# Attention and non-local layer: key differences renewed by a transfer or from the keys, a denser prologue, and a ScalarE copy of layer 1's denominators

## The chip, the cores and the metric

The program runs on one core of a Trainium2 chip. The metric is the device time of one execution in microseconds (us), as a median over runs. The engines are called as in the profile: PE (TensorE, matmuls), DVE (VectorE), ACT (ScalarE), POOL (GpSimd), SP (SyncE, which here only issues transfers). POOL and ACT issue transfers too.

## The reference

Two layers follow each other, all in float32, on x of 2 x 256 x 64 x 64 (two batches, 256 channels, 4096 positions).

```python
# layer 0: attention over 8 heads of 32 channels
qkv = jnp.einsum('oc,bchw->bohw', w_qkv, x)
q, k, v = map(reshape, jnp.split(qkv, 3, axis=1))        # b, 8, 32, 4096
scores = jnp.einsum('bhdi,bhdj->bhij', q, k) / sqrt(32)
out = jnp.einsum('bhij,bhdj->bhdi', softmax(scores), v)
x = jnp.einsum('oc,bchw->bohw', w_proj, out) + x
# layer 1: non-local block
g_x = maxpool2(conv1x1(x, g_w, g_b))                      # 256 channels, 1024 positions
theta_x = conv1x1(x[:, :64], theta_w, theta_b)            # 64 channels, 4096 positions
phi_x = maxpool2(conv1x1(x[:, 64:], phi_w, phi_b))        # 64 channels, 1024 positions
y = softmax(theta_x^T phi_x) applied to g_x
x = batchnorm(conv1x1(y, W_w, W_b)) + x
```

## The kernel before

**Tiling.** The eight heads of a batch are two quads of four heads (32 channels each, so a quad fills 128 partitions). `QUAD` counts them n = 0 to 3 over both batches: n = 0, 1 are batch 0, n = 2, 3 batch 1. A quad's 4096 queries are eight blocks of 512 (i = 0 to 7), and within a block a loop runs over 32 chunks of 128 keys (j = 0 to 31). For each block and j: `score` (line 452) makes the scores of the chunk in PSUM, ACT takes the exp (line 598) in two pairs of heads, `weigh` (line 476) multiplies the weights with v, and `add` sums the weights for the denominators: pair 0 by POOL (line 509, line 518 for the last chunk), pair 1 two chunks at a time by a transfer of 1 MB that adds in memory, issued by POOL (line 515). A block's two transferred sums are folded into one by another such transfer (line 524) and an addition (line 528), early in the next block. The weights stand in two rotating sets of buffers: `single` (six, for pair 0) and `double` (five, each two chunks of pair 1, or a running sum).

**Differences of keys.** The scores stay in PSUM from chunk to chunk: the matmul of chunk j adds q times the difference between chunk j's keys and those of the chunk before. In `keys` order the chunks walk over the eight stretches of 512 keys, so the differences needed are those between neighbouring stretches c = j % 8: odd c in `kd` (1, 3) and `last_kd` (5, 7), even c in `mid_kd` (2, 4, 6), and c = 0 in `turn_kd`. `kd` has two buffers; the other three have one and are renewed for the next quad when the last block of the quad before has read them for the last time. `between` makes one of mid_kd's three parts (128x512) on POOL, `rounds` makes turn_kd on POOL, `differences` makes one part of kd, first_kd or last_kd on POOL. `before_all` makes last_kd's content for the next quad early, in a tile `first_kd`, because the maxima (below) need it while the old last_kd is still read. `renew` does the renewals: mid_kd in the last block at j = 26, 28 and 30, turn_kd in the first block at j = 2, and two ACT copies first_kd to last_kd in the first block at j = 0 and 2.

first_kd has the tag "x" of a pool with one buffer, which the loads of x for q, k and v (x_q, x_k) and, at a batch's end, the weights of the projection and of two convolutions (`late_weights`, lines 103 to 107) also use.

**Maxima.** `maxima` finds the row maxima of the scores for a block ahead of its attention: about 4 chunks more than a block ahead. `plain` makes a product (line 293) that DVE reduces (line 305). `pair` uses differences: ACT takes a Relu of q times the difference (line 313), and DVE adds it to a product and reduces (line 320), which covers two stretches. The very first block's maxima are made by `first_block` in 33 slots, in the prologue, each with four products, two Relus (line 358) and two of DVE's joint reductions. `make_rows` turns finished maxima into rows by transposes on PE (line 150), which are subtracted in PSUM at j = 0 of a block (line 464).

**Prologue.** Ahead of the attention the program makes k, v and q of quad 0 from x (`make`, lines 185 and 197); these are the dense items, 14 of them after the first k, k, q. Four slots of the maxima follow each of k 2 to 7, v 0 and v 1; then come q(0,1) and v 2 to 7, with one step of the next block's maxima each.

**Batch end and layer 1.** `project` multiplies by w_proj (line 639), DVE adds x (line 646, from loads x_res, line 88, in `single` buffers); halfway it makes the last block's denominators (`den`, line 536). `non_local` makes theta, phi and g (lines 676 to 710) and then, per block of 512 positions i and for t = 0 to 3: scores (line 805), exp (line 820), the accumulation into two PSUM tiles (y, line 771) and sums on POOL (lines 763, 767), with maxima of later blocks (products line 739, reductions line 746) between. `result` then makes the denominators in a PSUM tile `den` (line 783), the reciprocal on DVE (line 785), and the output (lines 787, 790). The PSUM tiles y, y, den and pt (transposes) rotate over four buffers, and the program's waits follow the order in which they are given back.

**What sets the order.** The text of the loops gives the order; a scheduling layer orders each engine's instructions by priority, so that an instruction can stand earlier than in the text, and sets semaphores. `tc.issue_after` keeps an instruction behind another in that order.

Of the kernel before, what the change touches and what calls it, by code (L numbers as in the profile page):

```python
# [19 lines left out]
QUADS = HEADS // QH  # L20
# [5 lines left out]
NI = N // NB  # L26
NJ = N // P
# [8 lines left out]
def conv_attention(  # L36
# [13 lines left out]
    nc = tc.nc  # L50
# [116 lines left out]
    QUAD = [(b, qd) for b in range(B) for qd in range(QUADS)]  # L167
    q, k, v, kd = {}, {}, {}, {}
    held = {}

    def make(what, n, i):
        b, qd = QUAD[n]
        if (b, i) not in held:
            name = f"x_{what}_{n}_{i}"
            held.clear()
            held[b, i] = load_x(b, i, xs.tile([P, NC, NB], F32, tag="x", name=name))
        xc = held[b, i]
        name = f"{what}_{b}_{qd}_{i}"
        pq = scratch(name)
        if what == "v":  # L180
            if i == 0:
                v[n] = qkv.tile([P, NJ, QH, D], F32, tag="v", name=f"v_{n}")
            for j in range(NB // P):
                for c in range(NC):
                    nc.tensor.matmul(  # L185
                        pq[:, bass.ts(j, P)],
                        xc[:, c, bass.ts(j, P)],
                        wv_sb[:, c, bass.ts(qd, P)],
                        start=(c == 0),
                        stop=(c == NC - 1),  # L190
                    )
                if j % 2 == 1:
                    yield
            nc.scalar.copy(v[n][:, bass.ts(i, NB // P)].rearrange("p j h d -> p (j h d)"), pq)
            return
        for c in range(NC):
            nc.tensor.matmul(  # L197
                pq,
                wqk_sb[:, c, qd, 0 if what == "q" else 1, :],
                xc[:, c, :],  # L200
                start=(c == 0),
                stop=(c == NC - 1),
            )
            yield
        if what == "q":
            to = q[n, i] = qkv.tile([P, NB], F32, tag="q", name=f"q_{n}_{i}", bufs=3)
        else:
            if i == 0:
                k[n] = qkv.tile([P, N], F32, tag="k", name=f"k_{n}")
            to = k[n][:, bass.ts(i, NB)]  # L210
        nc.scalar.copy(to, pq)
        if what == "k" and i % 2 == 0 and i > 0 and n == 0:
            between(n, i // 2 - 1)
        if what == "k" and i == NI - 1 and n == 0:
            rounds(n)
        if what == "k" and i % 2 == 1 and n == 0:
            if i == 1:
                kd[n] = qkv.tile([P, NI // 4, NB], F32, tag="kd", name=f"kd_{n}")
            differences(n, i // 2, (kd[n] if i < NI // 2 else last_kd)[:, i // 2 % (NI // 4), :])
# [5 lines left out]
    def differences(n, c, to):  # L225
        two = k[n][:, bass.ts(c, 2 * NB)]
        nc.gpsimd.tensor_sub(to, two[:, NB:], two[:, :NB])
# [6 lines left out]
    def between(n, c):  # L234
        two = k[n][:, NB * (2 * c + 1) : NB * (2 * c + 3)]
        nc.gpsimd.tensor_sub(mid_kd[:, c, :], two[:, NB:], two[:, :NB])

    def rounds(n):
        nc.gpsimd.tensor_sub(
            turn_kd,  # L240
            k[n][:, P:NB].rearrange("p (a n) -> p a n", n=P),
            k[n][:, N - NB : N - P].rearrange("p (a n) -> p a n", n=P),
        )

    def renew(i, j, n):


        if (i, j) == (NI - 1, NJ - 6):
            between(n + 1, 0)
        elif (i, j) == (NI - 1, NJ - 4):  # L250
            between(n + 1, 1)
        elif (i, j) == (NI - 1, NJ - 2):
            between(n + 1, 2)
        elif (i, j) == (0, 2):
            rounds(n)
        if i == 0 and j in (0, 2):
            nc.scalar.copy(last_kd[:, j // 2, :], first_kd[n][:, j // 2, :])

# [146 lines left out]
    def advance(steps, n=1):  # L407
        for _ in range(n):
            next(steps, None)
# [3 lines left out]
    def make_rows():  # L413

        for i, r in enumerate(rows):
            if callable(r):
                if i in seen:
                    rows[i] = r()
                seen.add(i)


    def attend(b, y):
# [153 lines left out]
        for qd in range(QUADS):  # L576
            for i in range(NI):
                blk = Block(qd, i)
                items = during(blk.n, i)
                both = [None, None]  # L580
                for j in range(NJ):
                    if j % 2 == 0:
                        two = double(f"p_{blk.name}_{j}_1")
                    p = [single(f"p_{blk.name}_{j}_0"), two[:, j % 2]]
                    for pair in (1, 0):
                        if j == 0:
                            s = both[pair] = scores(f"s_{blk.name}_{j}_{pair}")
                            subtract(s, pair, blk)
                            advance(maxes)
                            score(s, pair, blk, j)  # L590
                        else:
                            s = both[pair]
                            score(s, pair, blk, j)
                            advance(maxes)
                        with ExitStack() as order:
                            if cut is not None:
                                order.enter_context(tc.issue_after(cut.ins))
                            nc.scalar.activation(p[pair], s, AF.Exp, scale=scale)  # L598
                    if waiting is not None:
                        weigh(*waiting)  # L600
                        if j == 0:
                            normal = normalize(waiting[0])
                    add(blk, j, p, two)
                    waiting = blk, j, p
                    if j in (1, 5) or j >= AFTER:
                        advance(normal)
                    if j % 2 == 0:
                        make_rows()
                        if i > 0 and blk.n + 1 < len(QUAD) or i == 0 and blk.n > 0:
                            with tc.issue_after(added.ins) if added else ExitStack():  # L610
                                renew(i, j, blk.n)
                        if i == NI // 2 and j in (12, 14) and blk.n + 1 < len(QUAD):
                            if j == 12:
                                kd[blk.n + 1] = qkv.tile(
                                    [P, NI // 4, NB], F32, tag="kd", name=f"kd_{blk.n + 1}"
                                )
                            with tc.issue_after(added.ins):
                                differences(blk.n + 1, j // 2 - 6, kd[blk.n + 1][:, j // 2 - 6, :])
                        if (i, j) == (NI - 1, 8) and blk.n + 1 < len(QUAD):
                            with tc.issue_after(added.ins):  # L620
                                before_all(blk.n + 1)
                    for item in items.get(j, ()):
                        if item[1] < len(QUAD):
                            advance(make(*item), 9)
# [28 lines left out]
    def non_local(b, y, theta_w, phi_w):  # L653
# [125 lines left out]
        def result(i):  # L779
            cols = bass.ts(i, NB)  # L780
            z = single(f"z_{b}_{i}")
            den = scratch(f"den1_{b}_{i}")
            nc.tensor.matmul(den, ones, acc[i][NC], start=True, stop=True)
            r = work.tile([P, NB], F32, tag="r", name=f"r1_{b}_{i}", bufs=1)
            nc.vector.reciprocal(r, den)  # L785
            for o in range(NC):
                nc.vector.scalar_tensor_tensor(
                    z[:, o, :], acc[i][o], bn_scale[:, o : o + 1], r, ALU.mult, ALU.mult
                )
                nc.vector.scalar_tensor_tensor(  # L790
                    z[:, o, :], z[:, o, :], bn_shift[:, o : o + 1], y[:, o, cols], ALU.add, ALU.add
                )
            nc.sync.dma_start(out=dst[:, :, cols], in_=z)
# [46 lines left out]
        held[0, i] = load_x(0, i, x0[:, :, bass.ts(i, NB)])  # L840
    for what, i in (("k", 0), ("k", 1), ("q", 0)):
        advance(make(what, 0, i), 3)
    for what, i in [("k", i) for i in range(2, NI)] + [("v", 0), ("v", 1)]:
        advance(make(what, 0, i), 3)
        advance(maxes, G)
    advance(maxes)
    advance(make("q", 0, 1), 3)
    for i in range(2, NI):
        advance(maxes)
        advance(make("v", 0, i), 3)  # L850
        if i in (3, 5):
            make_rows()
    advance(maxes, 2 * LEAD - NI + 2)
    held.clear()
    for b in range(B):
        y = big.tile([P, NC, N], F32, tag="y", name=f"y{b}")
# [58 lines left out]
```

## Time and profile before

| | |
|---|---|
| median of 3 runs | 3904.28 us (3903.01 to 3907.87) |
| profiled execution, own time | 3908.37 us |
| its span | 3906.6 us, granted clock 0.997 |
| PE busy | 3864.0 us (99%) |
| POOL busy | 3091.5 us (79%) |
| DVE busy | 2900.7 us (74%) |
| ACT busy | 2697.5 us (69%) |

Stages of the span, by the first exp of a quad and the first or last matmul of a stage: prologue to 99.3; quad 0 to 912.4; quad 1 to 1729.0; projection to 1768.6; layer 1 of batch 0 to 2019.6; quad 2 to 2839.5; quad 3 to about 3611; projection and layer 1 of batch 1 to the end.

In the profile, "PEld" is PE's weight load, "SPq" or "POOLq" an issue by that queue. In a row of the timeline the first number is the start, the second the duration, and the bracket the idle time before with what ended it. In a row of the chain the two numbers are start and duration of a piece; a DMA piece is the time in which the chain waits for a transfer. In "who waited for it" the two numbers are us in total and times.

### The profile page before, as it was taken

To read this page: it belongs to the slowest core of one execution; us is meant where nothing else is said; L and a number is where in the kernel's file an instruction comes from. 1 tells how busy PE (TensorE), PEld (TensorE's weight loads), DVE (VectorE), ACT (ScalarE), POOL (GpSimd) and SP (SyncE) were. 2 spreads that over 40 slices of the span, in tenths; PEclk is the share of its full clock that TensorE was granted. 3 is DMA by queue.
4 is the path that set the end of the run, shared out by engine and by line. 5 is a ranking of instruction groups with operands and counts; after the bars stand their busy time and mean duration, and the time that the engine had idled before them with its cause. 6 is when DMAs were issued, how large, how long until landed. Compare 5 with 4: busy or idle time off the path is not lost.

```text
span 3906.6 us, 69965 instructions
## 1 busy us (share of the span) xinstructions
PE 3864.0 (99%) x27452; PEld 1366.8 (35%) x27452; DVE 2900.7 (74%) x5449; ACT 2697.5 (69%) x3378; POOL 3091.5 (79%) x1957
## 2 busy tenths in 40 slices
PE   9999999999999999999999999999999999999998
PEld 4333333333333333333333333333333333332333
DVE  5888888788888888764458888888888888884444
ACT  5787777777777777751137777777778888887111
POOL 1888899899989999871448899998999999997043
PEclk9999999999999999999999999999999999999999
DMA  1778878778878788780018888887788888889100
GB/s 57 145 167 169 172 166 170 168 162 172 168 167 169 166 168 169 167 188 6 22 34 169 168 175 168 173 171 164 163 176 171 170 170 170 168 168 188 53 17 27
DMA packets 112300, 566.26 MB, mean 145 GB/s; under 512 B 20200, under 2 KB 22504, under 8 KB 50784
## 3 DMA queue, kind: packets, MB, share of 16 engines
q0 software_dynamic: 68832, 501.25, 63.5%
q1 hardware_dynamic: 42448, 59.74, 4.5%
q8 instruction: 215, 3.52, 0.3%
q14 instruction: 117, 0.96, 0.1%
q10 hardware_dynamic: 688, 0.79, 0.1%
HBM read 51.63 MB, written 8.88 MB: 15 GB/s over the span
## 4 chain that ended last, share of the span: by engine, by line
PE 96%; DVE 2%; DMA 1%; POOL 1%; issue 0%; ACT 0%; DVEq 0%; POOLq 0%; ACTq 0%; SPq 0%
PE s L452 28%; PE w L476 26%; PE ps L293 23%; PE y L771 6%; PE q L197 2%; PE k L197 2%; PE v L185 2%; PE proj L639 1%; PE g L696 1%; DVE r L785 1%; PE f L739 1%; PE f L805 1%; PE den L536 1%; DMA p<-p 1%; PE tp L680 0%; PE tp L676 0%
## 5 line engine op out<-in xcount | busy, mean ns | idle before, releaser
L509 POOL TENSOR_TENSOR p<-p,p 128x1024 f32<-128x1024 f32 x945 | 2364.4, 2502 | 281.4 <-ACT p L598 262.7
L598 ACT ACTIVATE p<-s 128x1024 f32<-128x1024 f32 x2048 | 2087.6, 1023 | 560.5 <-PE ps L293 495.1
L293 PE MATMUL ps<-k,q 32*128 32x512 f32 x6142 | 2020.6, 626 | 2.5 <-DVE r L785 1.3
L305 DVE TENSOR_REDUCE part<-ps 128x1 f32<-128x512 f32 x2046 | 1315.7, 686 | 566.8 <-PE ps L293 563.1
L476 PE MATMUL w<-p,v 128*32 128x512 f32 x8192 | 1091.0, 605 | 1.1 <-ACT p L598 1.1
L452 PE MATMUL s<-q,mid_kd 32*128 32x512 f32 x3072 | 771.2, 615 | 0.0
L320 DVE CUSTOM_DVE_ANT_0 ps<-ps,over 128x512 f32<-128x512 f32 x1025 | 706.2, 691 | 24.9 <-PE ps L293 10.5
L491 DVE TENSOR_TENSOR y<-y,w 128x512 f32<-128x512 f32 x961 | 659.1, 686 | 51.9 <-PE w L476 49.3
L293 PEld LDWEIGHTS ps<-k,q 32*128 32x128 f32 x6142 | 625.1, 183 | 25.6 <-DVE part L320 10.4
L313 ACT ACTIVATE over<-ps 128x512 f32<-128x512 f32 x961 | 569.3, 592 | 10.7 <-PE ps L293 7.9
L293 PE MATMUL ps<-kd,q 32*128 32x512 f32 x1056 | 525.9, 593 | 0.0
L452 PE MATMUL s<-q,last_kd 32*128 32x512 f32 x2048 | 508.5, 615 | 4.5 <-ACT p L598 4.5
L452 PE MATMUL s<-q,kd 32*128 32x512 f32 x2048 | 510.5, 616 | 0.4 <-ACT p L598 0.3
L293 PE MATMUL ps<-last_kd,q 32*128 32x512 f32 x904 | 445.1, 590 | 0.0
L476 PEld LDWEIGHTS w<-p,v 128*32 128x32 f32 x8192 | 161.6, 108 | 805.3 <-DVE part L305 775.2
L452 PEld LDWEIGHTS s<-q,mid_kd 32*128 32x128 f32 x3072 | 270.4, 183 | 443.5 <-ACT over L313 253.9
L515 POOL DMA_DIRECT2D p<-p x448 | 395.3, 882 | 27.3 <-ACT p L598 27.1
L452 PEld LDWEIGHTS s<-q,kd 32*128 32x128 f32 x2048 | 174.0, 184 | 299.8 <-ACT over L313 182.7
L452 PEld LDWEIGHTS s<-q,last_kd 32*128 32x128 f32 x2048 | 172.8, 183 | 284.9 <-ACT over L313 178.5
L771 PE MATMUL y<-p,kv 128*128 128x512 f32 x512 | 240.1, 608 | 6.4 <-DVE r L785 6.4
L820 ACT ACTIVATE p<-f 128x1024 f32<-128x1024 f32 x64 | 65.5, 1023 | 248.5 <-PE f L805 219.2
L767 POOL TENSOR_TENSOR sums<-sums,p 128x512 f32<-128x512 f32 x96 | 121.3, 1264 | 113.7 <-ACT p L820 109.9
(120 smaller groups left out, 2806.3 us busy)
## 6 DMA issues: line engine op xcount, KB each, us to landing
p<-p POOLq DMA_DIRECT2D x478, 1024.0 KB, 7.6
x_q<-in_x_dram SPq DMA_DIRECT2D x30, 512.0 KB
x_k<-in_x_dram SPq DMA_DIRECT2D x24, 512.0 KB
x_res<-in_x_dram SPq DMA_DIRECT2D x16, 512.0 KB
out_dram<-z SPq DMA_DIRECT2D x16, 512.0 KB
r<-flat SPq DMA_DIRECT2D x120, 64.0 KB
x<-in_x_dram SPq DMA_DIRECT2D x8, 512.0 KB
wqk_sb<-in_wqk_dram ACTq DMA_DIRECT2D x1, 512.0 KB
```

Of the source, the lines that this page charges most:

```text
L197: nc.tensor.matmul(pq, wqk_sb[:, c, qd, 0 if what == "q" else 1, :], xc[:, c, :], start=(c == 0), stop=(c == NC - 1),)
L293: nc.tensor.matmul(ps, q[n, i][bass.ts(h, D), bass.ts(g, P)], keys[bass.ts(h, D), :], start=True, stop=True,)
L305: reduced = nc.vector.tensor_reduce(part[:, g, h, j : j + 1], ps, AX.X, ALU.max)
L313: cut = nc.scalar.activation(over, ps, AF.Relu)
L320: reduced = nc.vector.tensor_tensor_reduce(out=ps, in0=ps, in1=over, scale=1.0, scalar=LEAST, op0=ALU.add, op1=ALU.max, accum_out=part[:, ...
L452: nc.tensor.matmul(s[:, t, :], kj[bass.ts(h, D), :], q[blk.n, blk.i][bass.ts(h, D), :], start=False, stop=True, skip_group_check=j > 0,)
L476: nc.tensor.matmul(w[bass.ts(h, D), :], v[blk.n][:, keys(j), h, :], p[h // 2][:, h % 2, :], start=True, stop=True,)
L491: nc.vector.tensor_add(blk.num, blk.num, w)
L509: added = nc.gpsimd.tensor_add(blk.sums[0], blk.sums[0], p[0])
L515: sent = nc.gpsimd.dma_start(out=blk.sums[n], in_=two, accum_op=ALU.add)
L598: nc.scalar.activation(p[pair], s, AF.Exp, scale=scale)
L771: nc.tensor.matmul(acc[i][o], wg[:, 2 * t + j, bass.ts(o, P)], p[:, j, :], **edge)
```

## The change

`renew` is rewritten. When the next quad is of the same batch (n = 0 to 1 and 2 to 3), mid_kd's first two parts are made as before at j = 26 and 28 of the last block; at j = 30 SP issues a transfer of first_kd's first part to last_kd; at j = 0 of the next quad's first block SP issues the second part's transfer and POOL makes mid_kd's third part; turn_kd is made at j = 4. When the next quad begins a batch (n = 2), POOL makes all of them from k: mid_kd, turn_kd and both parts of last_kd, given in the text at j = 0 of the first block; in the program's order they stand on POOL in the last block of quad 1, each after the last reading of the part that it overwrites. The ACT copies are gone. In the prologue three slots go with each of eleven items (k 2 to 7, v 0 to 4), then q(0,1), three items with one step each (v 5 to 7), and five steps without an item. In `result`, ACT copies den to the SBUF tile r in blocks i = 0 to 6, and the reciprocal works in place on r.

```diff
@@ -245,16 +245,24 @@
     def renew(i, j, n):
-        if (i, j) == (NI - 1, NJ - 6):
-            between(n + 1, 0)
-        elif (i, j) == (NI - 1, NJ - 4):
-            between(n + 1, 1)
-        elif (i, j) == (NI - 1, NJ - 2):
-            between(n + 1, 2)
-        elif (i, j) == (0, 2):
+        b, qd = QUAD[n]
+        if i == NI - 1 and qd < QUADS - 1:
+            if j in (NJ - 6, NJ - 4):
+                between(n + 1, (j - NJ + 6) // 2)
+            elif j == NJ - 2:
+                nc.sync.dma_start(out=last_kd[:, 0, :], in_=first_kd[n + 1][:, 0, :])
+        elif i == 0 and j == 0 and n > 0:
+            if qd > 0:
+                nc.sync.dma_start(out=last_kd[:, 1, :], in_=first_kd[n][:, 1, :])
+                between(n, 2)
+            else:
+                for c in range(NI // 2 - 1):
+                    between(n, c)
+                rounds(n)
+                for c in range(2):
+                    differences(n, NI // 4 + c, last_kd[:, c, :])
+        elif (i, j) == (0, 4) and qd > 0:
             rounds(n)
-        if i == 0 and j in (0, 2):
-            nc.scalar.copy(last_kd[:, j // 2, :], first_kd[n][:, j // 2, :])
@@ -606,9 +614,8 @@
                         make_rows()
-                        if i > 0 and blk.n + 1 < len(QUAD) or i == 0 and blk.n > 0:
-                            with tc.issue_after(added.ins) if added else ExitStack():
-                                renew(i, j, blk.n)
+                        with tc.issue_after(added.ins) if added else ExitStack():
+                            renew(i, j, blk.n)
@@ -782,6 +789,10 @@
             r = work.tile([P, NB], F32, tag="r", name=f"r1_{b}_{i}", bufs=1)
+            if i < NI - 1:
+                nc.scalar.copy(r, den)
+                den = r
             nc.vector.reciprocal(r, den)
@@ -840,17 +851,22 @@
-    for what, i in [("k", i) for i in range(2, NI)] + [("v", 0), ("v", 1)]:
-        advance(make(what, 0, i), 3)
-        advance(maxes, G)
+    slots = 2 * G * (NI // 2) + 1
+    for n, (what, i) in enumerate([("k", i) for i in range(2, NI)] + [("v", i) for i in range(NI)]):
+        if slots > 0:
+            advance(make(what, 0, i), 3)
+            advance(maxes, min(3, slots))
+            slots -= 3
+            if slots <= 0:
+                advance(make("q", 0, 1), 3)
+        else:
+            advance(maxes)
+            advance(make(what, 0, i), 3)
     advance(maxes)
-    advance(make("q", 0, 1), 3)
-    for i in range(2, NI):
-        advance(maxes)
-        advance(make("v", 0, i), 3)
-        if i in (3, 5):
-            make_rows()
-    advance(maxes, 2 * LEAD - NI + 2)
+    make_rows()
+    advance(maxes, 2)
+    make_rows()
+    advance(maxes, 2 * LEAD - 6)
```

## The prediction

> **What bounds the kernel now.** I read the page's busy times first, then the chain of waits in order of time, then single stretches of the timeline. TensorE is busy 99% of the span and carries 96% of the chain:
>
> ```profile
> PE 3864.0 (99%) x27452; PEld 1366.8 (35%) x27452; DVE 2900.7 (74%) x5449; ACT 2697.5 (69%) x3378; POOL 3091.5 (79%) x1957
> PE 96%; DVE 2%; DMA 1%; POOL 1%; issue 0%; ACT 0%; DVEq 0%; POOLq 0%; ACTq 0%; SPq 0%
> ```
>
> The change leaves TensorE's arithmetic as it is, so only time in which TensorE waits can move. In the stretch inside the attention the exps of successive key chunks j stand 2.96 us apart, and 20 of the 32 blocks repeat to 0.1 us (101.7 us a block in quads 0 to 2, 98.1 in quad 3). The exceptions stand in the chain as pieces that aren't TensorE's:
>
> ```profile
> 910.42 2.40 POOL p L509
> 913.37 1.85 issue
> 916.42 7.79 DMA p<-p
> 924.76 6.85 DMA p<-p
> ...
> 1727.57 7.14 DMA weights<-in_wproj_dram
> 1734.85 16.30 PE proj L639 x32
> 1751.15 3.57 PE den L536 x20
> ...
> 1856.94 3.37 DVE r L785
> ...
> 2843.39 9.98 DMA p<-p
> 2853.92 7.55 DMA p<-p
> ```
>
> Three places: the first block of quads 1 and 3 (about 912 and 2840), the end of batch 0's attention (1729), and layer 1 (DVE r, 14 times). The timeline of TensorE shows the second, with the idle time in brackets:
>
> ```profile
> 1728.97 1.06 PE L476 MATMUL w<-p,v 128*32 128x512 f32 x8 [1.14 <-ACT p L598]
> 1734.85 16.30 PE L639 MATMUL proj<-y,weights 128*128 128x512 f32 x32 [4.81 <-DMA weights<-in_wproj_dram]
> 1751.08 1.50 PE L536 MATMUL den<-p,ones 128*32 128x512 f32 x10
> ```
>
> and what waits for line 785 is
>
> ```profile
>   PEld y L771: 17.4, 14
>   PE y L771: 6.4, 14
> ```
>
> [...] after the 4.81 us gap six projection matmuls stand 0.85 us apart, the next ones 0.43. [...] Here 128x512 takes 3358 ns, a reduction of that size 686; from SBUF (line 547) it is 3354, so the copy doesn't shorten it. [...] the x_q load issued at 910.74 moves its first data at 915.5, when the accumulating transfer ahead of it is nearly through.
>
> **The change, part by part.**
>
> *1. Prologue.* Before, a dense item (k or v, 1.92 us of TensorE) and four score slots repeat every 7.35 us (35.92 to 43.26 at line 197's k). VectorE idles 1.40 us in each, then paces TensorE. The fourth slot is worth 1.31 us: the third slot's last matmuls end at about 41.9. Three slots and an item: 6.04 us. Eleven of them, less 0.76 for the quick first group: 65.7 us from 14.75, so q(0,1) starts at 80.4, not 74.46: **+5.9**. After it, before: q and a step to 78.18, six v of 1.98 with five steps between, to 95.58. After: 3.7, then three v and two steps (3 x 1.98 + 2 x 1.06 = 8.1), then three bare steps and the transposes, paced by VectorE (0.83 + 1.38 + 0.83 us of joints and reductions, about 3.2): 95.4. **Sum 0**; 0.2 us more or less per group gives -3 to +3.
>
> *2. Begin of quads 1 and 3.* Removed: two ACT copies (613 ns) in the last two chunks, which wait for TensorE's second score pair and stand ahead of exps; j=30 and 31 take 3.61 and 3.30 us there, against 3.29 and 3.09 in quad 3's blocks, which also carry no k and v items: 0.54. The larger loss is on POOL, which runs without a gap from 902 on: add, mid_kd (1.27), then DMA of the last pair, two adds; the fold of sums (line 524) must wait until that DMA has landed, and exp 6 waits for a double buffer that the fold frees, exp 8 for the add that follows (14.4 us after the fold's issue). These blocks cost 104.2 against 101.7 and 102.7 against 98.1; with the copies 3.1 and 5.2 us. After: mid_kd[2] stands behind that DMA, so it is issued 1.2 us earlier (915.2, 2842.2), on POOL's queue. SP gets two 256 KB transfers ahead of x_q. The second can't start before chunk 31's scores (910.4), runs behind the pair of j=28, at about 915.5, and x_q follows it into the hole between the last pair and the fold. So the last pair isn't shared with x_q (0.9 us at quad 1), nor with x_q and layer 1's two weight loads (9.98 us against 7.6 at quad 3): the fold starts at 922.6 and 2849.7 instead of 924.76 and 2853.92. POOL does the same work from there (turn_kd only moves behind two adds), so exp 8 gains **2.1** and **4.2**. Bounds: 1.2 and 2.5, if the small loads delay the fold; 2.6 and 4.7, if nothing waits. The transfers' own landing is needed at j=5 and j=7, 20 us after issue: nothing.
>
> *3. End of batch 0.* The weights' tile takes the buffer of first_kd. Before, its load waits for the second ACT copy, which ends at 1727.51; SP issues at 1727.57. After, quad 2's differences are made by POOL from k, and the last reader of first_kd is a maxima product that ends at 1711.2. SP then issues weights at about 1711.3, and they land before 1729. Saved: the 4.81 us gap, 2.6 of half clock (six matmuls at 0.85 instead of 0.43), 0.5 of the copies. Against it: POOL gains turn_kd (1.15) and two last_kd (2 x 1.27) in the last block; it runs without a gap there, so the last pair's DMA moves from 1733.1 to 1735.5 and the last add to end at 1740. den would be reached at 1743.1 and the DMA lands about 1743 to 1744.5. x_res loads wait for POOL's adds (1722.6 to 1735.8) and arrive as VectorE needs them. I take 0.7 back: **-7.2**; bounds -7.9 and -3.
>
> *4. Layer 1.* In the changed program the second accumulator (line 771's wait) waits for the ACT copy, about 0.6 us after den (an ACT copy of this size takes 0.585), not for 3.36. ACT is idle there from 1853.5 to 1858.9, when the exp queued behind the copy is due. Steps are 5.55 us apart, the one with the wait 6.29: 0.74 x 14, less 0.2 for a matmul that loses its hiding place at i=6: **-10.0**. What is late next: the reciprocal starts 0.66 later, so the reduction behind it (line 746) ends at 1862.1, and line 739 wants its buffer at 1862.3: just met. Bounds -10.4, and -3 if that fails by 0.5 us each time.
>
> Sum: 0 - 6.3 - 7.2 - 10.0 = **-23.5**. The profiled execution took 3908.37 us (span 3906.6), 4.1 above the median 3904.28; off the median the sum gives **3881**.
>
> **Rivals.**
> - The wait in layer 1 is renewed at line 739: the sum keeps 3 of 10 us, **3888**. For it: a margin of 0.2 us. Against it: the copy is all that is put before the reciprocal. 0.12.
> - At the end of batch 0 another transfer is late (the last pair for den, or x_res): 2.5 of 7.2 remain, **3886**. For it: 3.7 us more POOL work just there, and bursts on shared DMA engines. 0.13.
> - The prologue loses: denser items pay the 1.40 us refill eleven times, and the bare steps don't overlap: +6, **3887**. 0.08.
> - No change (within 0.2%, 7.8 us, about what a measurement of this kernel can tell): it takes two of these at once, **3900**. 0.04. That the copy would free nothing is excluded by the waits in the changed program.
> - Slower: last_kd's transfers land late, chunks 5 and 7 wait for them[...]. Slack is 20.7 us; the rest of the change gives 17, so each must land about 29 us after issue before it decides. At 35 us: 2 x (14 + 2.6) - 17 = +16, **3920**. For it: they queue behind 1 MB pairs. Against: the slowest pair took 9.98. 0.04.
>
> The likeliest case keeps 0.59. **Numbers:** 3881. All favourable bounds give 3876, and the runs shown spread by 5, so I begin at 3873; all unfavourable ones at once give 3898; I stop at 3894, which still holds the first three rivals: 3873 to 3894. Faster 0.91, same 0.05, slower 0.04.
>
> **What would show it.** Right: no TensorE gap before proj and full clock in it; line 771 without a wait for VectorE; folds at 922.6 and 2849.7 by today's clock; first exp near 99.3. Wrong: a new gap at den or at line 739, blocks of quads 1 and 3 as long as before, a first exp 3 us away.

## The result, and the profile after

The changed kernel takes 3888.20 us (median of 5 runs, 3884.94 to 3888.53), against 3907.87 us (3903.01 to 3912.77) for the kernel before on the same chip: ratio 0.9953, 95% interval 0.9943 to 0.9964, which is 14 to 22 us less. The prediction was 3881, with a range of 3873 to 3894 and a chance of 0.91 for faster. Its sum was -23.5 us, taken off 3904.28, the median of three earlier runs of the kernel before. Of the 7 us between 3881 and 3888.20, 3.6 lie in that start (3907.87 here) and 3.8 in the change, which is worth about -20; most of this second part lies in one of its four steps.

The profiled execution of after took 3884.94 us (span 3883.1), the shortest of its five. Of the page, the busy times and the chain's shares:

```profile
PE 3852.5 (99%) x27452; PEld 1361.3 (35%) x27452; DVE 2898.4 (75%) x5449; ACT 2702.5 (70%) x3386; POOL 3092.8 (80%) x1959
PE 96%; DMA 2%; POOL 1%; DVE 1%; issue 0%; ACT 0%; DVEq 0%; POOLq 0%; ACTq 0%
```

TensorE's share of the chain is still 96%, but DMA and DVE have changed places: 2% and 1%, where it was 1% and 2%. DVE's part is gone from layer 1; the chain in order of time shows what DMA gained (start, duration, what):

```profile
911.26 1.83 issue
913.09 10.17 DMA p<-p
923.30 0.48 issue
923.80 6.89 DMA p<-p
...
1733.90 9.66 DMA p<-p
1743.60 2.77 PE den L544 x12
...
2821.77 9.98 DMA p<-p
2837.10 7.71 DMA p<-p
```

Below, "the pair of j = 28" is the 1 MB transfer that adds chunks 28 and 29 of a block in memory, and "the last pair" the one for chunks 30 and 31; the fold of a block's two sums waits for the last pair. At quad 1 the last pair's transfer now holds the chain for 10.17 us instead of 7.79. The weights' piece (7.14 us at 1727.57) is gone. In TensorE's timeline the batch end reads

```profile
1728.43 14.00 PE L646 MATMUL proj<-y,weights 128*128 128x512 f32 x32
1742.37 1.06 PE L544 MATMUL den<-p,ones 128*32 128x512 f32 x8
1743.60 2.77 PE L544 MATMUL den<-p,ones 128*32 128x512 f32 x12 [0.17 <-DMA p<-p]
```

with no idle time in front of the projection and 14.00 us for its 32 matmuls, where it was 16.30. Those who waited for layer 1's reciprocal (us in total, times) are now only

```profile
L796 DVE RECIPROCAL r<-r x14: 3352/3353/3354, 1849.2 to 3855.3; 128x512 f32<-128x512 f32 x14
  PEld ps L301: 2.1, 1
  PE ps L301: 1.3, 1
  DVE z L798: 0.4, 2
```

The accumulator y (line 778, before line 771) is no longer among them. Blocks are counted 0 to 31 below, from the block's first exp to that of the next; blocks 8 and 24 are the first of quads 1 and 3, blocks 7 and 23 stand ahead of them. By place, in the two profiled executions:

| place | before | after | change | predicted |
|---|---|---|---|---|
| first maxima product to first exp | 82.74 | 81.45 | -1.3 | 0 |
| blocks 7 and 23 (the copies) | 98.67, 98.66 | 98.11, 98.11 | -1.1 | -6.3 for these three rows |
| block 8 | 104.21 | 106.01 | +1.8 | |
| block 24 | 102.68 | 101.29 | -1.4 | |
| block 15's first exp to the projection's second half | 124.03 | 116.44 | -7.6 | -7.2 |
| layer 1, first den to last reciprocal, two batches | 164.28 each | 159.07 each | -10.4 | -10.0 |

These make -20.0. Of the rest of the 23.4 us between the two profiled executions, 0.8 lie in the loads ahead of the first product and 1.6 at batch 1's end (block 31's first exp to the last projection matmul), a place that took 116.5 to 121.5 us over all kernels here, whatever their edit. The last 1.0 is block 16, right behind layer 1: it takes 106.1 to 106.3 us in the four kernels without layer 1's copy (before, e2, e3, e4) and 104.7 to 105.3 in seven of the nine with it (106.1 in e7, 108.0 in e11), so it may belong to the copy; no run shows how.

### The profile page after: what moved, and what is told of

It reads as the page before. It is cut to its first block, busy times and chain, and to the rows that moved or that the text cites. A ratio compares the mean times of both kernels' runs of the same rounds, so it can differ in the third digit from the quotient of the medians.

```text
span 3883.1 us, 69996 instructions
## 1 busy us (share of the span) xinstructions
PE 3852.5 (99%) x27452; PEld 1361.3 (35%) x27452; DVE 2898.4 (75%) x5449; ACT 2702.5 (70%) x3386; POOL 3092.8 (80%) x1959
## 4 chain that ended last, share of the span: by engine, by line
PE 96%; DMA 2%; POOL 1%; DVE 1%; issue 0%; ACT 0%; DVEq 0%; POOLq 0%; ACTq 0%
PE s L460 27%; PE w L484 26%; PE ps L301 23%; PE y L778 6%; PE q L197 2%; PE k L197 2%; PE f L746 2%; PE v L185 2%; DMA p<-p 2%; PE f L816 1%; PE g L703 1%; PE proj L646 1%; PE den L544 1%; PE tp L687 0%; PE tp L683 0%
```

## The experiments: one part at a time

**e1, layer 1's copy alone**, added to the kernel before:

```diff
+            if i < NI - 1:
+                nc.scalar.copy(r, den)
+                den = r
             nc.vector.reciprocal(r, den)
```

> The kernel before, with layer 1's copy of the denominator by ScalarE and nothing else. If the copy alone gives what the trace of after shows in layer 1 (-5.2 us in each batch), the profile loses 10.4 us in the two layer-1 stretches, line 771's product y no longer waits for VectorE, and all else stays: ratio about 0.9973. If the wait were renewed at the next maximum (the rival of the prediction), only 3 us would go. If layer 1's gain needed another part of the change (earlier loads), less than 8 us.

Measured: ratio 0.9973 (0.9963 to 0.9983), some 10.5 us. Both layer-1 stretches take 159.07 us, as in after, and y waits for no DVE. The copy alone gives it all; the next maximum doesn't wait.

**e2, the prologue alone**, added to the kernel before:

```diff
-        advance(make(what, 0, i), 3)
-        advance(maxes, G)
...
+        if slots > 0:
+            advance(make(what, 0, i), 3)
+            advance(maxes, min(3, slots))
+            slots -= 3
+            if slots <= 0:
+                advance(make("q", 0, 1), 3)
...
```

> The kernel before, with the denser items of the prologue alone. The trace of after has its first exp 2.1 us earlier, of which 0.8 is a quicker start that the edit doesn't touch. If the edit is worth what is left, the first exp comes 1 to 2 us earlier than before and the rest stays: ratio 0.9996. If its sum is zero, as predicted, the first exp is within 0.5 us of 99.3 once the time of the first product is taken off.

Measured: ratio 1.0001 (0.9992 to 1.0009), no difference that can be measured; in the trace 81.44 us from the first product to the first exp, as in after (81.45) and against 82.74 before and 82.73 in e1, where the prologue wasn't edited. So the edit is worth 1.3 us. The rest of the 2.1 was the start: the first product came between 15.27 and 16.56 us in before, after, e1 and e2.

**e3, quad 2's differences alone.** For n = 2 POOL makes mid_kd, turn_kd and last_kd from k; quads 1 and 3 keep their copies:

```diff
...
+        elif (i, j) == (0, 0) and n > 0 and qd == 0:
+            for c in range(NI // 2 - 1):
+                between(n, c)
             rounds(n)
...
+            for c in range(2):
+                differences(n, NI // 4 + c, last_kd[:, c, :])
...
-        if i == 0 and j in (0, 2):
+        if i == 0 and j in (0, 2) and qd > 0:
```

> The kernel before, with quad 2's differences made by GpSimd from the keys of batch 1, as in after; quads 1 and 3 keep their two copies. If the weights' load waited for the second copy and for nothing else, the 4.81 us gap ahead of the projection and its half clock go here too, and the projection begins right after the attention: -7.2 us predicted, about -7.7 seen in after, ratio 0.998. If the gain needs the transfers or the other parts, the gap stays at several us. Blocks 8 and 24 (the first of quads 1 and 3) stay at 104.2 and 102.7 us.

Measured: ratio 0.9983 (0.9976 to 0.9990), 4 to 9 us. The stretch to the projection's second half takes 116.95 us (before 124.03; 124.12 to 124.66 in e1, e2 and e4), and the gap is gone. Blocks 8 and 24 are 104.1 and 102.8. This part alone removes the gap: the weights' load waited for the second copy and for nothing else that lasted as long.

**e4, quads 1 and 3 alone**, quad 2 as before:

```diff
...
+            elif j == NJ - 2:
+                nc.sync.dma_start(out=last_kd[:, 0, :], in_=first_kd[n + 1][:, 0, :])
+        elif i == 0 and j == 0 and qd > 0:
+            nc.sync.dma_start(out=last_kd[:, 1, :], in_=first_kd[n][:, 1, :])
+            between(n, 2)
+        elif (i, j) == (0, 4) and qd > 0 or (i, j) == (0, 2) and qd == 0 and n > 0:
             rounds(n)
-        if i == 0 and j in (0, 2):
+        if i == 0 and j in (0, 2) and qd == 0 and n > 0:
```

> The kernel before, with the two transfers of last_kd and the moved GpSimd work at the begin of quads 1 and 3 alone; quad 2 keeps its copies. The prediction gave this part -6.3 us. If what after shows belongs to this part, block 8 is about 1.8 us longer than before and block 24 1.4 shorter, and the copies' 0.5 us go in each of the blocks ahead: about -0.6 us in all, no difference that can be measured. If after's long block 8 came of the other parts (all of the work there 2.6 us earlier against the transfers), block 8 is 102 here and the part gives -4 to -6 us.

Measured: ratio 1.0002 (0.9994 to 1.0010). Block 8 takes 106.00 us, block 24 101.35, blocks 7 and 23 98.11, all within 0.1 us of after. This part, for which the prediction counted 6.3 us, gives nothing that can be measured, and it does so alone: block 8's loss doesn't come from the other parts' earlier work.

## The experiments: why block 8 got longer

Theory A: between the pair of j = 28 and the fold (line 532, before line 524) the DMA engines have more to carry, and the fold is late. Theory B: the POOL work that was moved is at fault. SP's issues in after, at quad 1 and at quad 3 (start, duration, issue):

```profile
901.36 0.52 SPq L253 DMA_DIRECT2D last_kd<-first_kd  x1
907.62 0.49 SPq L256 DMA_DIRECT2D last_kd<-first_kd  x1
909.97 0.40 SPq L88 DMA_DIRECT2D x_q<-in_x_dram  x1
...
2822.09 0.50 SPq L256 DMA_DIRECT2D last_kd<-first_kd  x1
2831.98 0.40 SPq L88 DMA_DIRECT2D x_q<-in_x_dram  x1
2832.43 1.24 SPq L675 DMA_DIRECT2D g<-in_gw_dram  x1
2833.73 1.17 SPq L676 DMA_DIRECT2D g<-in_ww_dram  x1
```

x_q takes first_kd's buffer, so it starts when the second transfer has landed. By the packets of the trace, at quad 1 that transfer ran from 908.77 to 909.58, ahead of the pair of j = 28 (909.42 to 915.58); x_q ran from 914.76 to 917.49, and the last pair, issued at 913.09, from 916.50 to 922.98. POOL's timeline of after shows what the fold waited for:

```profile
917.27 2.62 POOL L517 TENSOR_TENSOR p<-p,p 128x1024 f32<-128x1024 f32 x1
923.80 0.87 POOL L532 DMA_DIRECT2D p<-p  x1 [3.91 <-DMA p<-p]
```

POOL was done and idle for 3.91 us until the pair landed. In before it was

```profile
924.76 0.87 POOL L524 DMA_DIRECT2D p<-p  x1 [2.78 <-DMA p<-p]
```

**e5, the transfers replaced by the two ACT copies**, POOL's order as in after:

```diff
-                nc.sync.dma_start(out=last_kd[:, 0, :], in_=first_kd[n + 1][:, 0, :])
...
-                nc.sync.dma_start(out=last_kd[:, 1, :], in_=first_kd[n][:, 1, :])
...
+        if i == 0 and j in (0, 2) and qd > 0:
+            nc.scalar.copy(last_kd[:, j // 2, :], first_kd[n][:, j // 2, :])
```

> The changed kernel with the two transfers of last_kd replaced by ScalarE's two copies, as before; GpSimd's order stays as changed. Theory A (block 8 is long because the DMA engines have more to carry between the pair of j=28 and the fold: 0.5 MB of last_kd, and x_q behind it): without the 0.5 MB, block 8 falls from 106.0 to 103.0 to 104.2 us and block 24 from 101.3 to 100 to 101.3, since x_q still meets the last pair; the copies cost 0.5 us in each block ahead. Theory B (the moved GpSimd work is at fault): block 8 stays within 0.4 us of 106.0. Ratio to before about 0.995 in either case, so the blocks decide.

Measured: block 8 103.94 us, so A. Block 24, however, is 102.77, longer than after's 101.29, which A's numbers didn't allow for. SP's issues of e5 at quad 3 show why:

```profile
2820.71 0.40 SPq L88 DMA_DIRECT2D x_q<-in_x_dram  x1
2824.45 0.40 SPq L673 DMA_DIRECT2D g<-in_gw_dram  x1
2824.89 0.85 SPq L674 DMA_DIRECT2D g<-in_ww_dram  x1
```

With the buffer free early, x_q and both weight loads go out ahead of the last pair (issued at 2825.11, first packet 2829.63); in after the late transfer keeps them back until 2832. At quad 3 the same delay of x_q that hurts at quad 1 moves more bytes out of the last pair's way. So transfers and copies come out even in the change as it stands: blocks 7, 8, 23 and 24 take 403.5 us in after and 404.1 in e5. Ratio to before 0.9953 (0.9941 to 0.9966).

**e6 and e7, last_kd made from k** by DVE (e6) or by POOL (e7), with no transfer and no copy:

```diff
+    def of_keys(n, c):
+        two = k[n][:, bass.ts(NI // 4 + c, 2 * NB)]
+        nc.vector.tensor_sub(last_kd[:, c, :], two[:, NB:], two[:, :NB])   # e7: nc.gpsimd
...
-                nc.sync.dma_start(out=last_kd[:, 0, :], in_=first_kd[n + 1][:, 0, :])
+                of_keys(n + 1, 0)
...
-                nc.sync.dma_start(out=last_kd[:, 1, :], in_=first_kd[n][:, 1, :])
+                of_keys(n, 1)
```

> The changed kernel with last_kd of quads 1 and 3 made by VectorE from the keys: no transfer and no copy, and first_kd is free earlier, so x_q can load in the hole ahead of the pair of j=28. Theory A: nothing is left on the DMA engines beside the pairs, the fold is issued about 2.4 us earlier after the block's begin; block 8 about 103.6 us, block 24 about 99.5; against the changed kernel -4 us, ratio to before about 0.994. Theory B: block 8 stays at 106.0. A third outcome: VectorE stalls behind the subtraction, which waits for the last scores of the block, and the block ahead or block 8 gets longer than 106.

> The changed kernel with last_kd of quads 1 and 3 made by GpSimd from the keys: the same relief for the DMA engines as with VectorE, but 1.27 us more of GpSimd in the chain at each of the two places. Theory A: block 8 is 103.6 plus 1.3 to 2.5, so 104.9 to 106.1; block 24 100.8 to 102. Theory B would make it longer than 106.5, since GpSimd's own chain decides. Against the same work on VectorE it shows what a GpSimd instruction costs here.

Measured: e6 0.9949 (0.9936 to 0.9961), e7 0.9953 (0.9940 to 0.9967). In e6 the fold is issued 10.6 us after block 8's begin (after: 14.0) and the block waits for it nowhere; but j = 0 takes 5.19 us, and j = 30 of the block ahead 4.56 instead of 3.29, so block 8 is 103.92, near A's 103.6, and block 7 1.3 longer; block 24 is 100.28 (A's 99.5). DVE's stall of the third outcome is there, though no block gets longer than 106, and it isn't a wait for scores (last section). e7 has 104.59 and 102.69: at quad 1 a little under A's 104.9 to 106.1 and far from B's 106.5, at quad 3 over A's 102, where quad 3's weight loads went out at 2826.72, ahead of the last pair (2829.14), as in e5.

**e8, x_q held back, transfers kept.**

```diff
+                        if (i, j) == (0, 6) and blk.n > 0 and blk.qd > 0:
+                            held.clear()
+                            late = xs.tile([P, NC, NB], F32, tag="x", name=f"x_q_{blk.n}_2")
+                            with tc.issue_after(added.ins):
+                                nc.gpsimd.memset(late[:, 0, :1], 0.0)
+                            held[b, 2] = load_x(b, 2, late)
```

> The changed kernel with its two transfers kept, but the load x_q for quads 1 and 3 held back until the fold has landed (a one-column write of its buffer by GpSimd, behind the add of j=6, has to come first). Theory A: the last pair no longer shares the engines with x_q's 0.5 MB (nor, at quad 3, with the two weight loads behind it on SP's queue): the fold is issued 0.9 to 1.3 us earlier after the block's begin, block 8 about 105.0, block 24 about 100. If the transfers of last_kd alone make the loss, block 8 stays at 106.0. If x_q comes too late for its product at j=11, j=11 gets longer than 4.87 us.

Measured: ratio 0.9946 (0.9934 to 0.9959). Block 8 falls to 103.33 us, 2.7 less than after and more than the 1.0 expected; without x_q between them the two pairs run back to back (909.96 to 920.57), and POOL's idle time ahead of the fold shrinks from 3.91 to

```profile
921.65 0.87 POOL L532 DMA_DIRECT2D p<-p  x1 [1.24 <-DMA p<-p]
```

j = 11 stays at 4.87 us, so x_q, issued at 938.66, comes in time. Block 24 gets longer (102.83): the weight loads, no longer behind x_q, go out at 2824.21, among the pairs. The expectation missed that.

**e9, as e8, the weight loads of quad 3 held back too:** POOL writes two columns of the weights' tile behind the add of j = 6, and the loads must wait for that.

```diff
...
+                        if (i, j) == (0, 6) and blk.n == len(QUAD) - 1:
+                            early[b] = qkv.tile([P, NC * (M + 2 * C)], F32, tag="v", name=f"g_{b}")
+                            with tc.issue_after(added.ins):
+                                nc.gpsimd.memset(early[b][:, NC * (M + C) - 1 : NC * (M + C) + 1], 0.0)
```

> The changed kernel with x_q held back until the fold has landed (as in e8) and, in quad 3, layer 1's two weight loads as well. From the kernels so far block 8 is 101.67 us plus what the fold's issue is later than 9.67 us after the block's first exp (after 14.0, e5 11.9, e7 12.6, e8 11.35). Theory A2 (the DMA engines' load between the pair of j=28 and the fold decides, whichever transfer it is): block 8 stays at e8's 103.3; block 24, freed of the weight loads too, has its fold 11.4 us after its begin and takes 99.8 us instead of 102.8 in e8 and 101.3 in the changed kernel; about -4 us against the changed kernel, ratio to before 0.9942. Rival: quad 3's block is long for another reason (its POOL chain): 102 to 103.

Measured: ratio 0.9943 (0.9931 to 0.9956). Block 8 103.40 as expected; block 24 101.39, not 99.8, though 1.4 less than in e8. What is left there is the second transfer: it is issued at 2819.22 and its packets lie scattered among those of the two pairs until 2828.55, and the pairs take 13.1 us together (2820.38 to 2833.45), against 10.7 at quad 1; in e10, without the transfer, they take 11.6 at quad 3.

**e10, as e9 with the ACT copies** instead of the transfers, by e5's edit:

```diff
-                nc.sync.dma_start(out=last_kd[:, 1, :], in_=first_kd[n][:, 1, :])
...
+            nc.scalar.copy(last_kd[:, j // 2, :], first_kd[n][:, j // 2, :])
```

> As e9, and last_kd copied by ScalarE instead of by the two transfers: only the pairs are left on the DMA engines. The difference to e9 is what the transfers cost. Prediction of this case: nothing. By A2 the second transfer's 0.25 MB, which e8's packets show just ahead of the pair of j=28, holds that pair up by 0.5 to 1.0 us: block 8 102.4 to 102.9 and block 24 98.9 to 99.4 here; the copies take 0.54 in each block ahead, so the whole time is that of e9 within 1 us.

Measured: ratio 0.9940 (0.9927 to 0.9954). Block 8 takes 102.47 us, as expected, and block 24 99.83, a little over; that is 0.9 and 1.6 less than e9, and the copies give back 0.56 and 0.66 in blocks 7 and 23. So with the loads held back the transfers cost more than the copies that they replace, by 1.3 us for the four blocks. The profile puts e10's wait ahead of the fold at quad 1 down to an exp:

```profile
921.14 0.87 POOL L533 DMA_DIRECT2D p<-p  x1 [0.90 <-ACT p L607]
```

The exp is no new limit, though. The trace has the last pair's landing at 920.60, and the fold is issued 0.54 us after it; in before, after, e5, e8 and e9 it is also issued 0.54 us after that landing. The transfer still sets it.

**e11, as e6, the subtractions moved** behind DVE's sums of chunks 31 and 1 (`done` collects these), quad 3's weight loads held back as in e9:

```diff
...
+        with tc.issue_after(done[-1].ins):
+            nc.vector.tensor_sub(last_kd[:, c, :], two[:, NB:], two[:, :NB])
...
+                of_keys(n, 0)      # at (0, 0)
+        elif (i, j) == (0, 2) and qd > 0:
+            of_keys(n, 1)
```

> As e6 (last_kd by VectorE from the keys), with the two subtractions moved behind VectorE's sums of chunks 31 and 1, so that they no longer wait for scores, and quad 3's weight loads held back. In e6 the subtraction's wait held VectorE: j=30 took 4.56 instead of 3.29 us and j=0 5.19 instead of 3.01. If that stall was e6's loss, both go back to 3.3 and 3.0, the fold is issued about 11 us after block 8's begin and the block takes 102.5 to 103.1; block 24 99 to 99.5; ratio to before about 0.994. If the later subtractions come too late for chunks 5 and 7, a new wait stands at j=4 to 7 ahead of the fold's.

Measured: ratio 0.9944 (0.9932 to 0.9957). j = 30 and j = 0 are back at 3.29 and 3.01, block 24 takes 99.82 and block 8 103.35, both 0.3 us over their ranges: j = 1 and j = 3 of block 8 each take 0.8 us more than their 2.96.

**One rule for block 8.** Times from the block's first exp:

| kernel | last packet of the last pair | fold issued | block 8 | 101.67 + fold - 9.67 |
|---|---|---|---|---|
| before | 11.2 | 12.3 | 104.21 | 104.3 |
| after | 13.2 | 14.0 | 106.01 | 106.0 |
| e5, copies | 11.1 | 11.9 | 103.94 | 103.9 |
| e7, POOL | 11.5 | 12.6 | 104.59 | 104.6 |
| e8, x_q late | 10.2 | 11.3 | 103.33 | 103.3 |
| e9, x_q and weights late | 10.3 | 11.4 | 103.40 | 103.4 |
| e10, and copies | 9.4 | 10.5 | 102.47 | 102.5 |

101.67 is an undisturbed block; 9.67 was fitted on after, e5, e7 and e8 before e9 and e10 were run, and this one number serves seven kernels within 0.1 us. Each microsecond by which the fold is issued later than that costs a microsecond. e6 and e11 lie 1.3 and 0.4 over the rule, by DVE's own delays. At quad 3 it holds less well (0.3 off in e10, 0.9 in e7).

**The best version.** Blocks 7, 8, 23 and 24 take 404.2 us before, 403.5 after, 401.0 in e9, 399.7 in e10 and 399.5 in e11. By their ratios to before (0.9943, 0.9940 and 0.9944) e9, e10 and e11 lie under after's 0.9953, but the intervals overlap: the 4 us are shown by the traces, not by the times.

## Why the prediction was right, and where it was off

- **Prologue, 0 predicted, -1.3 measured.** The mis-sized term is the period: the eleven groups took 64.3 us (from the k at 13.99 to q(0,1) at 78.25) and not 65.7; items stand 11.75 us apart by twos (k at 19.16 and 30.91 us), so 5.87 each instead of 6.04. Within the -3 to +3 given.
- **Begin of quads 1 and 3, -6.3 predicted, -0.7 measured: the step that failed.** The copies' 0.54 (0.55), the role of the fold and the earlier issue of the last pair (915.2 and 2842.1 by before's clock, as forecast) were right. Wrong was "runs behind the pair of j=28, at about 915.5, and x_q follows it into the hole between the last pair and the fold". At quad 1 the transfer ran ahead of that pair, whose first packet came 1.97 us after its issue instead of 1.43, and x_q, released by the landing, ran ahead of the last pair. "So the last pair isn't shared with x_q" was the opposite of what happened: the pair is issued 0.7 us earlier after the block's begin and lands 2 us later. The fold was forecast at 922.6; it comes at 923.80 in a run that begins block 7 2.1 us earlier than before, so at 925.9 by before's clock, 1.1 later than before's 924.76. At quad 3 the fold gains 2.1 us by the same reckoning (2851.8), where 4.2 were forecast (2849.7), because x_q and the weight loads were kept behind the last pair, but the transfer ran among the pairs. The bounds, 1.2 and 2.5 us of gain at the least, allowed for small loads that delay the fold, not for a longer wait than before; the measured 0.7 for both places lies outside their sum of 3.7. "The transfers' own landing ...: nothing" held for their readers; what their bytes cost the pairs is 0.9 and 1.6 us (e9 against e10).
- **End of batch 0, -7.2 predicted, -7.6 measured.** By before's clock (this run begins block 15 0.76 us earlier) the weights' load is issued at 1711.4 (predicted 1711.3), den is reached at 1743.1 (1743.1) and the last pair has landed by 1744.4 (1743 to 1744.5). Two terms were too large: half clock cost 2.3 us (16.30 to 14.00), not 2.6, since in before the matmuls behind the gap start 0.99, four times 0.85 and once 0.58 us apart, not six times 0.85 (the trace of before has the granted clock at half from 1732.71 to 1739.54, from inside the 4.81 us gap to 4.7 us after the first of them at 1734.85; in after it is 1.00 throughout the 14.00 us); and of the 0.7 us taken back, 0.17 was there.
- **Layer 1, -10.0 predicted, -10.4 measured.** The wait went from the whole reciprocal (3.36 us for 128x512) to the copy of 0.585 us, and nothing new stands at the next maximum.

The measured terms make -20.0; the ratio says -18.4, with -14 to -22 as its interval. Of the rivals, the renewed wait in layer 1 and the late transfer at the batch end didn't occur, nor did the prologue lose. The "slower" rival looked at the transfers' landing, 20 us before they are read; what they delayed were the pairs and the loads behind them, which the prediction had placed elsewhere. That 3888.20 lies in the range is in part luck: step 2 missed its own bounds, and the range held because the bounds of the other three steps, which were met, left room for it. That three rivals stood at 3886 to 3888 is chance as well, since none of the three occurred.

## What to carry to other kernels

A copy that is handed from a busy engine to a transfer is not free just because nobody waits for its data: ask which transfers its buffer holds back, and where these then fall among the others (blocks 8 and 24 were 0.9 and 1.6 us longer with the two transfers than with copies, e9 against e10). Loads of 0.5 MB like x_q belong where no large transfer is on the way to a waiter (holding x_q back took 2.7 us off block 8, e8); a write of one column by the engine that knows the time (e8 to e10) is enough to hold them there. And where a block's length follows one event, here the fold, plot the one against the other over a few kernels: the rule then prices each next edit.

## What the runs showed of the hardware

**DVE's subtraction ends at a fixed time after POOL's addition.** The subtraction of two 128x512 operands from SBUF took 1.32 to 2.52 us in e6, where DVE's sum y of the same size, with one operand in PSUM, takes 0.69. DVE's and POOL's timelines of e6:

```profile
909.40 2.52 DVE L247 TENSOR_TENSOR last_kd<-k 128x512 f32<-128x512 f32 x1
```

```profile
908.72 5.42 POOL L521 TENSOR_TENSOR p<-p,p 128x1024 f32<-128x1024 f32 x2
```

The first of the two additions ends at 911.37; the subtraction, begun in its midst, ends at 911.93, 0.56 us after that. In e11 the same holds again (DVE, then POOL):

```profile
919.31 1.39 DVE L248 TENSOR_TENSOR last_kd<-k 128x512 f32<-128x512 f32 x1
```

```profile
917.49 2.65 POOL L522 TENSOR_TENSOR p<-p,p 128x1024 f32<-128x1024 f32 x1
```

The addition ends at 920.14, the subtraction at 920.70. All eight subtractions of e6 and e11 (1.22 to 2.52 us) begin inside an instruction of POOL and end 0.55 to 0.57 us after it. There is no idle time in front of any of them, so e6's stall was not the wait for scores that its expectation, and e11's, supposed.

A control is in every kernel: in the last block DVE has 15 additions of its own with two operands from SBUF. Two of before's, and POOL beside them:

```profile
3575.64 1.23 DVE L507 TENSOR_TENSOR p<-p,p 128x1024 f32<-128x1024 f32 x1
3580.85 1.89 DVE L507 TENSOR_TENSOR p<-p,p 128x1024 f32<-128x1024 f32 x1
```

```profile
3575.15 0.88 POOL L515 DMA_DIRECT2D p<-p  x1
3578.07 2.35 POOL L509 TENSOR_TENSOR p<-p,p 128x1024 f32<-128x1024 f32 x1 [2.04 <-ACT p L598]
3580.39 1.26 POOL L568 TENSOR_TENSOR y<-y,w 128x512 f32<-128x512 f32 x1
```

Over all 13 traces, 134 of these additions begin while POOL has no arithmetic under way and take 1.22 to 1.23 us. The other 61 begin inside an instruction of POOL, take 1.26 to 1.93, and every one ends 1.08 to 1.09 us after POOL's. So where they begin inside an instruction of POOL, subtractions and additions each end at their own fixed time after it; what joins the two engines was not shown. TensorE paid for it one step later in e6, by a product that waited 1.36 us for DVE's next reduction:

```profile
912.65 1.12 PE L305 MATMUL ps<-kd,q 32*128 32x512 f32 x2 [1.36 <-DVE part L332]
```

**What sharing costs a 1 MB transfer.** With only the pairs on the way (e10) the packets of each run for 5.2 us (909.23 to 914.45, 914.88 to 920.06); beside x_q and last_kd in after they run for 6.2 and 6.5. A load of 0.5 MB issued behind a pair moved its first data only when the pair was nearly through: x_q waited from 909.97 to 914.76 in after, and from 908.11 to 912.87 in e5. Why the second last_kd transfer runs ahead of the pair at quad 1 and scattered through it at quad 3, in each of after, e4, e8 and e9, is left open. One reading fits. Where the transfer runs ahead, its first packet comes 1.15 us after its issue; where the pair goes first, its first packet comes 1.42 to 1.44 us after its own. By the difference of these two, an estimate, the transfer would be first if it is issued less than about 0.28 us after the pair. It is issued 0.12 to 0.17 us after it at quad 1 and 0.26 to 0.32 at quad 3 (a tie, within 0.02 us, in e9). No run moved the issue, so this isn't shown.
